# Checking adj's entries: every second row tile by GpSimd and ScalarE, and the diagonal by one strided transfer

## The chip, the cores and the metric

The kernel runs on one core of a Trainium2 chip. The metric is the device time of one execution in microseconds (us). Engines are named as the profile names them: PE is TensorE, DVE is VectorE, ACT is ScalarE, POOL is GpSimd, SP is SyncE, which issues most of the transfers.

## The reference

Four graph layers run one after the other on x, 8 batches of 2048 nodes with 64 features, each as `x = x + layer(relu(layernorm(x)))`. Cut to what matters here:

```python
# x: (8, 2048, 64), adj: (2048, 2048)
h = jnp.maximum(_layernorm(x, axis=-1), 0.0)
x = x + layer0(h, H, adj, ...)     # adj / max(adj.sum(-1), 1) times a projection of h,
                                   # mixed with a hypergraph attention over H
h = jnp.maximum(_layernorm(x, axis=-1), 0.0)
x = x + layer1(h, adj, ...)        # I, A and 2 A A - I as a Chebyshev basis
h = jnp.maximum(_layernorm(x, axis=-1), 0.0)
x = x + layer2(h, adj, ...)        # three rounds of adj times v, each with a small network
h = jnp.maximum(_layernorm(x, axis=-1), 0.0)
x = x + layer3(h, adj, ...)        # attention: softmax over all nodes of adj * leaky_relu(e),
                                   # with adj's diagonal set to 1
```

adj holds only zeros and ones (a sparse random graph whose diagonal is 1). The reference doesn't depend on that, but the kernel has a short path that does.

## The kernel before, in words

The launch has two parts. `start` does the first layernorm, multiplies its result by layer 0's weight in two layouts, and checks the inputs. It ends in a flag: 0 where adj holds only zeros and ones and no node has more neighbours than the short path has room for. `tc.nc.values_load(flag, ...)` reads it, and an `If` takes the short path or the long one (`rest(True)` or `rest(False)`). The whole of each branch is behind that read, on every engine. The profile shows the short path: the first instructions behind the flag start at 111.2 us, and the four layers fill the rest of the span.

Within `start`:

- `layernorm_relu` (called at its end through `norm_parts`, lines 258 to 281) goes over 4 chunks of 512 nodes. A chunk is one 1 MB load `x_ch`, then for each of 4 pairs of batches a matmul with `center`, an ACT Square into `sq` (L264), and a relu into `xr`, in turn on DVE (L267) and on ACT (L269); then a matmul that sums the squares, ACT's square root (L272), DVE's reciprocal (L273), four matmuls that spread the result, and four multiplications by DVE (L553). `xr`, `sq` and `std` have one buffer each, so that a chunk's parts follow those of the chunk before; six banks of PSUM are shared by all matmuls of the stage.
- `features` goes over the same 4 chunks: 4 matmuls 128x512 into `ph` and 4 groups of four 128x128 matmuls into `pn`, each result copied out of PSUM by `copy`, which takes ACT (L172) and DVE (L174) in turn. It starts when the layernorm has given its banks back.
- `check_adj` (L339) goes over the 16 tiles of 128 rows of adj, 1 MB each. SP loads a tile into one of four places (`rows`, two buffers of two tiles, L351). DVE multiplies its 128 columns on the diagonal by the identity and sums them, which gives each node's own entry (`own`, L352). ACT squares the tile into one of two places of `squares`, and sums the squares into `deg` (L357). DVE compares the tile with its squares, writes the comparison over them, and sums it into `same` (L358): an entry is 0 or 1 exactly where it equals its square. `bad` is set where the sum is short of 2048 x 16 over the row's tiles (L362, L363), and `own` becomes deg minus the own entry (L364).
- `count_nodes` turns the degrees of H and adj into counts of nodes above given sizes, and compares them with the room that the short path has (L371 to L407); the rest of `start` joins the three flags over the partitions (L561 to L566).

An instruction of DVE or ACT that also gives a sum shows in the profile with a second, short one that reads the accumulator.

Nothing in the source gives an order between the layernorm, the features and the check. The tile framework arranges each engine's queue when the program is built, and each engine then works through its queue in that order; so check instructions stand among those of the layernorm and the features on SP, ACT and DVE. A place of `rows` is loaded again when its last reader is done, four tiles later, and a place of `squares` is written again two tiles later.

Of the kernel before, what the change touches and what calls it, by code (L numbers as in the profile page):

```python
# [7 lines left out]
F = mybir.dt.float32  # L8
# [4 lines left out]
AF = mybir.ActivationFunctionType  # L13
OP = mybir.AluOpType
# [5 lines left out]
P = 128  # L20
NB = 8
N = 2048
D = 64
NP = NB // 2
NT = N // P
# [102 lines left out]
class Kernel:  # L128
# [210 lines left out]
    def check_adj(self, pool, slots):  # L339


        nc = self.nc
        rows = [slots.tile([P, 2, N], F, name=f"rows{i}", tag=f"q{6 + i}") for i in range(2)]
        squares = slots.tile([P, 2, N], F, name="squares", tag="q8")
        same = pool.tile([P, NT], F, name="same")
        deg = pool.tile([P, NT], F, name="deg")
        own = pool.tile([P, NT], F, name="own")
        junk = pool.tile([P, P], F, name="junk")
        for t in range(NT):
            row, sq = rows[t // 2 % 2][:, t % 2], squares[:, t % 2]  # L350
            nc.sync.dma_start(row, self.a["adj"][t * P : (t + 1) * P])  # L351
            nc.vector.scalar_tensor_tensor(  # L352
                junk, row[:, t * P : (t + 1) * P], 1.0, self.ident, op0=OP.mult, op1=OP.mult,
                accum_out=own[:, t : t + 1],
            )

            nc.scalar.activation(sq, row, AF.Square, accum_out=deg[:, t : t + 1])  # L357
            nc.vector.scalar_tensor_tensor(  # L358
                sq, row, 1.0, sq, op0=OP.mult, op1=OP.is_equal, accum_out=same[:, t : t + 1]
            )  # L360
        bad = pool.tile([P, 1], F, name="bad")
        nc.vector.tensor_reduce(bad, same, axis=AX.X, op=OP.add)  # L362
        nc.vector.tensor_scalar(bad, bad, float(N * NT), None, op0=OP.is_lt)  # L363
        nc.vector.tensor_sub(own, deg, own)  # L364
        return bad, deg, own
# [1985 lines left out]
```

## Time and profile before

| what | us |
|---|---|
| median of 3 runs | 2163.15 |
| the 3 runs | 2158.54, 2163.15, 2169.57 |
| the profiled execution | 2161.53 |
| its span, first to last instruction | 2159.8 |
| DVE busy in the span | 1133.9 |
| ACT busy in the span | 712.2 |
| POOL busy in the span | 706.0 |
| last load of a tile of adj issued by the check | 65.0 |
| the flag's last instruction | 110.35 |

The span is counted from the first instruction to the last; the execution's time has a little around it. The views give start times from the span's start. A row of the timeline reads: start, duration, engine, line, operation, written<-read, shapes, number, and in brackets the idle time of the engine before it and what ended it. Neighbouring instructions of a queue overlap by a tenth or two of a us at their ends, so the cost of one in a row of several is the distance between starts. A group's row gives busy time and mean nanoseconds of one, then the idle time before its instructions and its releasers.

### The profile page before, as it was taken

The page shows a single profiled execution, that of the slowest core. Times are in us where ns is not written, and L with a number is a line of the kernel's source. Part 1 is how long each engine was busy: PE and PEld are TensorE (multiplying, and loading weights), DVE is VectorE, ACT ScalarE, POOL GpSimd, SP SyncE. Part 2 cuts the span into 40 slices and gives each one's busy share as a digit, 9 for nine tenths or more (in the row PEclk, how much of TensorE's full clock was granted, in tenths as well). Part 3 has the DMA queues.
Part 4 walks back from the last instruction along what each step waited for, and adds up shares of the span by engine and source line. Part 5 has one row for each costly group of instructions (what it writes and reads, how often), then busy time and mean ns, then how long its engine had stood idle before and what let it go on. Part 6 is the DMA issues. An engine that isn't in the chain of part 4 may idle for free. (4 is left out here: it accounts for less than half of the span.)

```text
span 2159.8 us, 21301 instructions
## 1 busy us (share of the span) xinstructions
PE 1945.0 (90%) x7466; PEld 1163.0 (54%) x7466; DVE 1133.9 (53%) x1956; ACT 712.2 (33%) x1343; POOL 706.0 (33%) x595
## 2 busy tenths in 40 slices
PE   5879999978879999999999998899999999669885
PEld 1425766642237774353453543677777666445433
DVE  7877677736661123425434255698703222248774
ACT  6412555534543440020110201324335333248400
POOL 0000467754310005707447166011000000177870
PEclk8868999987769999999999999999999999879997
DMA  8230333441024460050230500556444444375665
GB/s 318 82 109 6 103 104 116 134 166 39 40 80 126 123 175 31 5 151 1 73 83 0 122 1 28 169 176 223 167 125 129 135 149 147 132 221 166 177 184 183
DMA packets 108796, 253.64 MB, mean 117 GB/s; under 512 B 20912, under 2 KB 21056, under 8 KB 101376
## 3 DMA queue, kind: packets, MB, share of 16 engines
q1 hardware_dynamic: 89264, 181.45, 27.0%
q0 software_dynamic: 17104, 66.47, 10.1%
q10 hardware_dynamic: 2304, 4.20, 0.5%
q8 instruction: 62, 1.02, 0.2%
q14 instruction: 62, 0.51, 0.1%
HBM read 218.30 MB, written 33.78 MB: 117 GB/s over the span
## 5 line engine op out<-in xcount | busy, mean ns | idle before, releaser
L325 ACT CAST adj<-adj_t 128x512 fp32r<-128x512 f32 x384 | 237.4, 619 | 687.2 <-PE pp L166 354.7
L1408 POOL TENSOR_TENSOR acc<-acc,y 128x512 f32<-128x512 f32 x224 | 277.2, 1269 | 449.2 <-DVE y L1403 449.2
L166 PE MATMUL pp<-adj,hi 128*128 128x512 f32 x1280 | 365.6, 405 | 0.1
L166 PE MATMUL pk<-q,w 128*128 128x512 f32 (+1 forms) x1024 | 358.2, 611 | 4.3 <-ACT q L1376 3.0
L166 PE MATMUL pp<-adj,lo 128*128 128x512 f32 x1280 | 358.7, 400 | 0.0
L166 PEld LDWEIGHTS pp<-adj,hi 128*128 128x128 f32 x1280 | 242.1, 191 | 72.4 <-issue 16.0
L166 PEld LDWEIGHTS pp<-adj,lo 128*128 128x128 f32 x1280 | 244.0, 191 | 56.5
L166 PEld LDWEIGHTS pk<-q,w 128*128 128x128 f32 (+1 forms) x1024 | 136.5, 188 | 214.1 <-issue 167.3
L1403 DVE SCALAR_TENSOR_TENSOR y<-pk,bias,q 128x512 f32<-128x512 f32 x224 | 157.7, 746 | 142.0 <-PE pk L166 135.7
L166 PE MATMUL acc<-q,ident 128*128 128x512 f32 x416 | 202.9, 614 | 26.4 <-DVE q L2138 16.5
L2048 POOL DMA_INDIRECT ring<-f_rows,near x121 | 139.7, 1154 | 67.0 <-issue 28.0
L166 PEld LDWEIGHTS acc<-q,ident 128*128 128x128 f32 x416 | 76.7, 194 | 102.4 <-issue 47.2
L2152 POOL IOTA q<- 128x2048 int32 x1 | 1.8, 1834 | 316.5 <-PE p L166 316.5
L166 PE MATMUL pp<-adj,x_ind_hi 128*128 128x512 f32 x256 | 94.7, 486 | 2.2 <-DVE q L738 1.9
L1840 POOL TENSOR_TENSOR q<-q,beta 128x512 f32<-128x512 f32 x57 | 67.9, 1193 | 54.6 <-DVE beta L1816 30.8
L1403 DVE SCALAR_TENSOR_TENSOR acc<-pk,bias,q 128x512 f32<-128x512 f32 x32 | 22.6, 747 | 119.9 <-PE pk L166 119.9
L166 PE MATMUL bank<-std,from_rows 32*128 32x512 f32 x128 | 46.7, 894 | 41.9 <-DVE std L273 33.8
L2119 DVE TENSOR_TENSOR q<-ring,e 128x1024 f32<-128x1024 f32 x58 | 70.1, 1219 | 8.9 <-PE acc L166 8.8
L166 PE MATMUL pp<-adj,x_ind_lo 128*128 128x512 f32 x256 | 71.7, 399 | 0.0
L1530 POOL DMA_INDIRECT q<-in_adj_dram,order x15 | 19.0, 1270 | 160.3 <-DVE top L1544 133.5
L166 PEld LDWEIGHTS pp<-adj,x_ind_hi 128*128 128x128 f32 x256 | 48.5, 189 | 38.9 <-issue 23.7
L1495 DVE SCALAR_TENSOR_TENSOR q<-p,cols,q 128x512 f32<-128x512 f32 x16 | 12.0, 751 | 108.4 <-PE p L166 107.5
(411 smaller groups left out, 2768.4 us busy)
## 6 DMA issues: line engine op xcount, KB each, us to landing
adj_t<-in_adjT_dram SPq DMA_DIRECT2D x128, 512.0 KB, 4.0
adj_t<-in_adjT_dram SPq DMA_DIRECT2D x128, 256.0 KB, 3.3
rows<-in_adj_dram SPq DMA_DIRECT2D x16, 1024.0 KB, 5.6
q<-x SPq DMA_DIRECT2D x10, 1024.0 KB, 4.9
x<-q SPq DMA_DIRECT2D x9, 1024.0 KB, 3.9
q<-in_embT_dram SPq DMA_DIRECT2D x8, 1024.0 KB, 11.5
x_ch<-in_xT_dram SPq DMA_DIRECT2D x4, 1024.0 KB, 6.3
h_rows<-q SPq DMA_DIRECT2D x16, 256.0 KB, 3.6
```

Of the source, the lines that this page charges most:

```text
L166: self.nc.tensor.matmul(out, lhsT, rhs, start=start, stop=stop)
L325: nc.scalar.copy(moving, at[:, i])
L1403: nc.vector.scalar_tensor_tensor(y, pks[b, half], bias[:, b : b + 1], emb[:, b], op0=OP.add, op1=OP.mult,)
L1408: nc.gpsimd.tensor_add(acc, acc, y)
L1495: nc.vector.scalar_tensor_tensor(x[:, q], p2, self.col("b2"), x[:, q], op0=OP.add, op1=OP.add)
L1530: nc.gpsimd.indirect_dma_start(row, None, self.a["adj"], bass.IndirectOffsetOnAxis(ap=order[:, 1, t : t + 1], axis=0),)
L1840: self.nc.gpsimd.tensor_tensor(x, x, by.unsqueeze(2).to_broadcast([P, NB, D]), op=OP.mult)
L2048: self.nc.gpsimd.indirect_dma_start(to, None, self.kern.f_rows[:], bass.IndirectOffsetOnAxis(ap=index, axis=0))
L2119: nc.vector.tensor_tensor(y.rearrange("n i (b f) -> n i b f", b=NB), block[:, i : i + 2, : NB * D].rearrange("n i (b f) -> n i b f", b=NB) ...
L2152: nc.gpsimd.iota(whole, pattern=[[1, N]], base=0, channel_multiplier=0)
```

## The change

Even tiles are treated as before. For an odd tile, GpSimd subtracts the squares from the tile, in place of the squares, and ScalarE sums the absolute values of the difference into `differ`, which is 0 for a row exactly where all its entries equal their squares. That second ScalarE instruction (`total`) is placed in the source ahead of the load of the tile two further on, which takes the same place of `squares`. At the end, a row of an odd tile with a zero in `differ` counts 2048, as a full comparison did, and is added to the even tile's `same`. The own entries no longer come from the loaded tiles: one transfer issued by GpSimd reads adj's diagonal from memory, 128 x 16 single f32 entries 2049 entries apart, into `own`, at the head of the check. The buffer `junk` is gone, and `same` has half its columns.

```diff
-        same = pool.tile([P, NT], F, name="same")
+        same, differ = (pool.tile([P, NT // 2], F, name=n) for n in ("same", "differ"))
         deg = pool.tile([P, NT], F, name="deg")
         own = pool.tile([P, NT], F, name="own")
-        junk = pool.tile([P, P], F, name="junk")
+        adj = self.a["adj"]
+        nc.gpsimd.dma_start(
+            own, bass.AP(tensor=adj.tensor, offset=adj.offset, ap=[[N + 1, P], [P * (N + 1), NT]])
+        )
+
+        def total(t):
+            sq = squares[:, t % 2]
+            nc.scalar.activation(sq, sq, AF.Abs, accum_out=differ[:, t // 2 : t // 2 + 1])
+
         for t in range(NT):
             row, sq = rows[t // 2 % 2][:, t % 2], squares[:, t % 2]
+            if t % 2 and t > 2:
+                total(t - 2)
             nc.sync.dma_start(row, self.a["adj"][t * P : (t + 1) * P])
-            nc.vector.scalar_tensor_tensor(
-                junk, row[:, t * P : (t + 1) * P], 1.0, self.ident, op0=OP.mult, op1=OP.mult,
-                accum_out=own[:, t : t + 1],
-            )
 
             nc.scalar.activation(sq, row, AF.Square, accum_out=deg[:, t : t + 1])
-            nc.vector.scalar_tensor_tensor(
-                sq, row, 1.0, sq, op0=OP.mult, op1=OP.is_equal, accum_out=same[:, t : t + 1]
-            )
+            if t % 2 == 0:
+                nc.vector.scalar_tensor_tensor(
+                    sq, row, 1.0, sq, op0=OP.mult, op1=OP.is_equal,
+                    accum_out=same[:, t // 2 : t // 2 + 1],
+                )
+            else:
+                nc.gpsimd.tensor_sub(sq, row, sq)
+        total(NT - 1)
         bad = pool.tile([P, 1], F, name="bad")
+        none = pool.tile([P, NT // 2], F, name="none")
+        nc.vector.tensor_scalar(none, differ, 0.0, float(N), op0=OP.is_equal, op1=OP.mult)
+        nc.vector.tensor_add(same, same, none)
         nc.vector.tensor_reduce(bad, same, axis=AX.X, op=OP.add)
```

## The prediction

> **What bounds the kernel now.** The change lies in the first 111 us, before the flag that the program branches on. I first cut that stretch into windows (us; busy time of each engine with its number of instructions; TensorE clock; DMA share; GB/s):
>
> ```profile
> 18.00:82.00 64.00, 40.38 (x101) 13.02 (x102) 63.60 (x88) 42.00 (x55) 0.00 (x0) 0.76 0.69 255
> 82.00:105.30 23.30, 23.30 (x143) 17.54 (x142) 14.01 (x58) 7.85 (x14) 0.00 (x0) 1.00 0.00 1
> 105.30:111.20 5.90, 0.80 (x5) 0.12 (x2) 4.67 (x45) 0.00 (x0) 0.00 (x0) 0.98 0.01 1
> ```
>
> The busy columns are PE, PE's weight load, DVE, ACT, POOL. From 18 to 82 us DVE works 63.60 of 64.00 us: it bounds the layernorm and the check, which share the stretch. From 82 to 105.3 us PE works all the time (the features). Then comes a tail on DVE that makes the flag. POOL does nothing. Next the groups of the first 110 us:
>
> ```profile
> L358 DVE SCALAR_TENSOR_TENSOR squares<-rows,squares 128x2048 f32<-128x2048 f32 x16 | 36.5, 2282 | 1.2 <-ACT squares L357 1.2
> L357 ACT ACTIVATE squares<-rows 128x2048 f32<-128x2048 f32 x16 | 30.5, 1907 | 15.2 <-DVE squares L358 13.9 <-DMA rows<-in_adj_dram 1.3
> L273 DVE RECIPROCAL std<-std 128x512 f32<-128x512 f32 x4 | 13.4, 3349 | 0.7 <-ACT std L272 0.7
> L352 DVE SCALAR_TENSOR_TENSOR junk<-rows,ident 128x128 f32<-128x128 f32 x16 | 4.4, 274 | 1.5 <-DMA rows<-in_adj_dram 1.5
> ```
>
> The check (L352, L358) is about 41 of DVE's us here, and ACT waits 13.9 us for it. How that delays the layernorm is in DVE's timeline of chunk 1 (start, duration):
>
> ```profile
> 34.85 3.34 DVE L273 RECIPROCAL std<-std 128x512 f32<-128x512 f32 x1
> 38.11 0.23 DVE L352 SCALAR_TENSOR_TENSOR junk<-rows,ident 128x128 f32<-128x128 f32 x1
> 38.26 0.08 DVE L352 DVE_READ_ACCUMULATOR junk<-rows,ident 128x1 f32 x1
> 38.26 2.29 DVE L358 SCALAR_TENSOR_TENSOR squares<-rows,squares 128x2048 f32<-128x2048 f32 x1
> 40.47 0.08 DVE L358 DVE_READ_ACCUMULATOR squares<-rows,squares 128x1 f32 x1
> 40.47 0.28 DVE L352 SCALAR_TENSOR_TENSOR junk<-rows,ident 128x128 f32<-128x128 f32 x1
> 40.68 0.08 DVE L352 DVE_READ_ACCUMULATOR junk<-rows,ident 128x1 f32 x1
> 40.68 2.29 DVE L358 SCALAR_TENSOR_TENSOR squares<-rows,squares 128x2048 f32<-128x2048 f32 x1
> 42.90 0.08 DVE L358 DVE_READ_ACCUMULATOR squares<-rows,squares 128x1 f32 x1
> 42.90 2.48 DVE L553 TENSOR_TENSOR q<-xr,bank 128x512 f32<-128x512 f32 x4
> ```
>
> Two whole tiles of the check stand between the reciprocal and the multiplications of L553, which PE's first matmul would have released some 0.7 us after 38.11: L553 is 4.1 us late. The same 4 us is lost in each chunk, and the reciprocals of chunks 1 and 2 begin 2.1 us after their square root. The reciprocals start at 18.34, 34.85, 51.33 and 65.79: periods of 16.5, 16.5 and 14.5, mean 15.8. The last L553 ends at 76.1.
>
> **What the Trainium skill says.** SBUF — State Buffer, section "Who interferes with whom": a VectorE instruction with two inputs in SBUF and a GpSimd instruction that reads SBUF exclude each other; the later one waits for the whole of the earlier. The trace agrees, in a later stage:
>
> ```profile
> 505.43 2.69 POOL L660 TENSOR_TENSOR dt<-tanh 128x1024 f32<-128x1024 f32 x1 [3.54 <-ACT tanh L658]
> 506.44 2.24 DVE L670 TENSOR_TENSOR df<-q,q 128x512 f32<-128x512 f32 x1
> ```
>
> L670 takes 0.69 at other times; here it lasts until 0.56 after POOL's end. GPSIMD Engine Reference, section "3.1 Elementwise": a two-input f32 operation on 2048 elements takes 4497 ns. The trace has none of that length, but 1.26 us for 512 elements (shortest L666) and 2.34 for 1024 (L660): 1.08 more per 512, so 2.34 + 2 x 1.08 = 4.50. ScalarE: Activation LUTs, section "Table sets", has abs in every table set, so Abs adds no table load; no run here shows that yet. DMA: Bandwidth & Descriptors, section "Queues, rings and completion order": each DMA engine takes turns between queues by packets, so a transfer of POOL's gets among SP's; this trace has no such meeting at its start.
>
> **The change part by part.**
>
> DVE loses eight L358, 2.21 from start to start (38.26 to 40.47), 17.7 us, and sixteen L352 at 0.21 (40.47 to 40.68), 3.4: 21.1 us. The two small instructions at the end (0.16 each, like L362 and L364) lie beside the features and cost nothing; if the check were last they'd cost 0.3.
>
> POOL gains eight subtractions of 4.50, 36 us on an idle engine. Unobstructed they're free; what they do to DVE is the lock. In a steady pair of tiles ACT squares the odd one, POOL starts, ACT squares the even one 1.9 later, and DVE's L358 then waits 4.5 - 1.9 = 2.6 and works 2.2: 4.8, with whatever DVE has queued behind it, L553 or the reciprocal, waiting too. Before, a pair took 2 x (2.21 + 0.21) = 4.84. So where the instructions meet, DVE's saving is gone; where they don't, all of it stays.
>
> ACT gains eight Abs at 1.89 (34.68 minus 32.79, two squares in a row): 15.1. It worked 48.7 us between 10 and 82 (42.0 of 64 in the window above, the rest ahead of it), so it comes to 63.8 of 72. Slot 1 of squares has now a chain: square 1.9, subtraction 4.5, Abs 1.9, with 0.2 for hand-overs 8.5 per odd tile, 68 for eight, from about 17 to 85 us; with a wait or two on ACT and the lock, 95. The flag's tail starts at 105 now, so this chain alone isn't last.
>
> What sets the stretch is the layernorm's chain, with ACT's queue in it. Its bare period: reciprocal 3.3, first matmul and four L553 3.1, PE and ACT to the square root's end about 4.9: 11.3. In chunks 2 and 3 the trace has the burst of squares to the square root's end unbroken, 44.92 to 49.27 = 4.4. From the root to the next burst a bare chunk leaves ACT 6.4 to 6.9 us (11.3 less 4.4), and that is where the check's ACT work is queued now, four squares of 1.9. With the same sort of order after the change: square odd, square even, a wait to 6.4 for POOL, Abs, square odd: 10.3, a period of 14.7. With one instruction less behind the wait it is 8.4, a period of 12.8. An instruction on ACT that waits for POOL holds the layernorm's squares behind it, and PE and DVE wait for those. I can't tell from the trace which order is built, and take 14.0, a little nearer to the longer one. Three periods: 3 x (15.8 - 14.0) = 5.4. After the last reciprocal, 65.79 to 76.1 = 10.3 becomes 3.35 + 0.7 + 2.4 and one L358 of 2.2, 8.6: 1.7 saved.
>
> The diagonal's transfer: 2048 pieces of 4 bytes. For its issue on POOL the nearest row is an indirect transfer of 128 rows, 0.95; sixteen times that is 15.2, and POOL isn't wanted before 18: nothing, at either end. For the DMA engines the nearest is hm<-in_H_dram, 2048 runs of 256 bytes, 6.4 us to landing. It would go out near 2 us, together with the first x_ch (issued 2.50, used at 8.02), which the whole chain waits for. Between 0 and 6.4. x_ch is 512 runs of 2 KB, 32 for each of 16 engines, the diagonal 128 for each; turn by turn 32 of those 128, a quarter of 6.4, get in before x_ch is through: I take 1.5. It can't be a gain: nothing is taken out of the queues there.
>
> The features keep their 29.4 us of PE (75.57 to 105.0). Two or three pairs of the check fall beside them; before, two L358 did (76.24 and 79.26) with PE still busy. I put 0, at worst 2 per pair, 6.
>
> The sum: 5.4 + 1.7 - 1.5 = 5.6. All engines wait for the flag, so an earlier flag moves the end by as much. The profiled execution took 2161.5 (span 2159.8), 1.6 below the median 2163.15. 2161.5 - 5.6 = 2155.9; for the median, 2157.6.
>
> **The rivals.**
> Full gain: the built order fits, no lock is met, the period falls to 11.3, 3 x 4.5 = 13.5, and the end to 6.4 (3.9), the transfer hidden: 17.4 less. The squares' chain, 85 to 88, still ends in time. 2146. For it: DVE has no idle time now, and loses a third of its work. Against it: ACT at 63.8 of 72.
> The lock eats it: 4.8 against 4.84 per pair, and the transfer's 1.5: 2164.6. For it: L670 above.
> Slower: two odd tiles' chains are queued on ACT between a root and the next squares, 2 x 8.5 = 17, a period of 21.4, 5.6 more, three times 16.8, less 1.7, plus 1.5: 2179.8. It costs from the point where the gap is over 15.8 - 4.4 = 11.4, that is 1.3 odd tiles per gap. Against it: a full pair a gap is all that eight pairs in some 80 us need.
>
> **How the numbers follow.** Forecast 0.50, full gain 0.18, lock 0.20, slower 0.12. 0.5% is 10.8 us, about what a measurement here can tell from no change (the runs span 2158.5 to 2169.6). Faster by more: the full gain and 0.04 of the forecast, 0.22. Slower by more: two thirds of the last, 0.08. The rest, 0.70, is within. The range runs from the full gain's 2146 to 2170, which takes in the lock with features worsened by 6; half of the full gain and most of the slower case stay out.
>
> **What would show it.** Right: the reciprocals 13 to 15 us apart, POOL's subtraction at 4.5 us or more, some L358 stretched past 2.29, ACT idle on POOL's squares, the last L553 near 70, the flag near 105. Periods under 12 show the full gain; L358 near 4.8 on average shows the lock; ACT's wait for POOL above 20 us with squares of the layernorm behind it shows the slower case. A first x_ch later than 9.5 shows the transfer mis-sized. I'd be wrong altogether if the flag came early and the end didn't.

## The result and the profile after

The changed kernel takes 2177.59 us, median of 11 runs (2170.59 to 2184.35), against 2162.8 for the kernel before in as many runs beside it. The ratio is 1.007, with a 95% interval from 1.0052 to 1.0088: slower, by some 15 us, where the forecast was 5.6 us faster. The profiled execution took 2179.18 us, 17.6 more than the one of before, with a span of 2177.4.

First, where the time went. The flag's last instruction starts at 127.61 us in place of 110.35, 17.3 later. That is all but 0.3 of the difference of the two profiled executions; behind the flag nothing changed (2049.5 and 2049.8 us). So the three windows of before are cut again at the same events: first reciprocal to last multiplication, features, tail (busy columns PE, PE's weight load, DVE, ACT, POOL):

```profile
19.60:93.00 73.40, 39.24 (x85) 11.17 (x85) 55.65 (x57) 54.08 (x66) 33.35 (x8) 0.74 0.61 220
93.00:122.50 29.50, 29.50 (x158) 21.68 (x159) 15.91 (x45) 10.59 (x17) 3.22 (x1) 0.90 0.00 1
122.50:128.40 5.90, 0.86 (x4) 0.09 (x2) 4.67 (x45) 0.00 (x0) 0.00 (x0) 0.83 0.01 1
```

Features and tail are as long as before, 29.5 and 5.9 us. The first window grew, and in it DVE now works 55.65 of 73.40 us: it has idle time again, and the stretch got longer. Whatever bounds it now, it isn't DVE's work.

The layernorm's reciprocals start at 19.61, 39.38, 58.47 and 77.61 (before: 18.34, 34.85, 51.33, 65.79), periods of 19.8, 19.1 and 19.1, mean 19.3 where it was 15.8. The last multiplication ends at 92.9 (76.1). So: first reciprocal 1.3 later, three periods 10.5, the end after the last reciprocal 15.3 instead of 10.3, so 5.0, and the features 0.5: 17.3.

Next the groups of the first 128 us that answer to those of before:

```profile
L371 POOL TENSOR_TENSOR squares<-rows,squares 128x2048 f32<-128x2048 f32 x8 | 36.6, 4572 | 56.7 <-ACT squares L364 56.7
L366 DVE SCALAR_TENSOR_TENSOR squares<-rows,squares 128x2048 f32<-128x2048 f32 x8 | 22.4, 2798 | 6.3 <-ACT squares L364 6.3
L356 ACT ACTIVATE squares<-squares 128x2048 f32<-128x2048 f32 x8 | 15.2, 1905 | 18.8 <-POOL squares L371 18.8
L379 DVE TENSOR_TENSOR own<-deg,own 128x16 f32<-128x16 f32 x1 | 3.4, 3446 | 0.0
```

The sizes were as forecast: the subtraction 4572 ns, the sum (L356) 1905, the comparison (L366) 2282 before and 2798 on the mean now, because two of the eight met a subtraction (4.82 us at 66.17, 4.03 at 34.81). The new row is the 18.8 us that ACT waits in front of L356 for POOL, in five waits: one in each of the three gaps between a root and the next chunk's squares (4.62, 4.88 and 2.74), two after the last root. ACT's timeline in the gap ahead of chunk 2, between the root of chunk 1 (L272) and chunk 2's squares (L264), shows one of them (start, duration; in brackets the idle time ahead of the instruction):

```profile
38.03 0.69 ACT L272 ACTIVATE std<-bank,eps 128x512 f32<-128x512 f32 x1 [1.25 <-PE bank L166]
38.62 1.90 ACT L356 ACTIVATE squares<-squares 128x2048 f32<-128x2048 f32 x1
...
40.51 1.90 ACT L364 ACTIVATE squares<-rows 128x2048 f32<-128x2048 f32 x1
...
42.40 1.90 ACT L364 ACTIVATE squares<-rows 128x2048 f32<-128x2048 f32 x1
...
49.27 1.91 ACT L356 ACTIVATE squares<-squares 128x2048 f32<-128x2048 f32 x1 [4.88 <-POOL squares L371]
...
51.30 1.91 ACT L364 ACTIVATE squares<-rows 128x2048 f32<-128x2048 f32 x1
...
53.21 1.06 ACT L264 ACTIVATE sq<-bank 128x512 f32<-128x512 f32 x2
```

The subtraction that it waits for, from POOL's timeline:

```profile
44.47 4.77 POOL L371 TENSOR_TENSOR squares<-rows,squares 128x2048 f32<-128x2048 f32 x1 [7.78 <-ACT squares L364]
```

From the root's end, 38.72, to the next squares, 53.21, are 14.5 us. In them ACT sums an odd tile, squares an even one, squares the next odd one, and then has the sum of that odd tile at its queue's head. POOL began that subtraction at 44.47 and takes 4.77, so ACT stands for 4.88 us, and the layernorm's squares stand behind it; when their turn comes they start without a wait of their own. The gap ahead of chunk 3, from 58.43 to 72.82, holds six instructions of the check (square, sum, square, square, sum, square), 14.4 us. The one ahead of chunk 1 holds four and a wait, 12.2 us, and a fifth stands among chunk 1's squares.

Last, what a subtraction does to a small instruction. The timeline of all engines at the end of the layernorm:

```profile
83.03 4.95 DVE L386 TENSOR_SCALAR least<-deg 128x16 bf16<-128x16 f32 x7
83.06 4.51 POOL L371 TENSOR_TENSOR squares<-rows,squares 128x2048 f32<-128x2048 f32 x1 [5.55 <-ACT squares L364]
...
87.90 0.67 DVE L568 TENSOR_TENSOR q<-xr,bank 128x512 f32<-128x512 f32 x1
```

Seven instructions on 16 elements took 4.95 us, one of them 4493 ns, where the median of the eleven between 83.0 and 88.7 is 161: it ended with POOL's subtraction. The multiplication behind them, which starts the features, came 4.9 us later than DVE's turn for them.

### The profile page after: what moved, and what is told of

Its sections match the earlier page's. It is cut to its first block, busy times and chain, and to the rows that moved or that the text cites. A ratio compares the mean times of both kernels' runs of the same rounds, so it can differ in the third digit from the quotient of the medians.

```text
span 2177.4 us, 21278 instructions
## 1 busy us (share of the span) xinstructions
PE 1944.5 (89%) x7466; PEld 1161.2 (53%) x7466; DVE 1123.2 (52%) x1910; ACT 728.2 (33%) x1359; POOL 745.5 (34%) x604
## 5 line engine op out<-in xcount | busy, mean ns | idle before, releaser
L166 PE MATMUL acc<-q,ident 128*128 128x512 f32 x416 | 203.0, 614 | 28.6 <-DVE q L2153 18.3
L1545 POOL DMA_INDIRECT q<-in_adj_dram,order x15 | 19.1, 1270 | 158.8 <-DVE top L1559 132.4
L1855 POOL TENSOR_TENSOR q<-q,coef 128x512 f32<-128x512 f32 x57 | 59.6, 1045 | 26.3 <-DVE q L1878 21.2
```

What stands on the lines that cost most here:

```text
L166: self.nc.tensor.matmul(out, lhsT, rhs, start=start, stop=stop)
L1545: nc.gpsimd.indirect_dma_start(row, None, self.a["adj"], bass.IndirectOffsetOnAxis(ap=order[:, 1, t : t + 1], axis=0),)
L1855: self.nc.gpsimd.tensor_tensor(x, x, by.unsqueeze(2).to_broadcast([P, NB, D]), op=OP.mult)
```

## The experiments

Sixteen kernels were run. Since the difference lies ahead of the flag, each is read by three numbers of its profile, beside the ratio of its time to that of the kernel before: the mean period of the reciprocals, the last multiplication's end, and the time from the first reciprocal to the flag ("stretch"), which leaves out how early the first loads came. The ratio is of many runs beside the kernel before; the other three are of one execution each. In those of the experiments the part behind the flag took 2059 to 2077 us (e14 aside), against 2050 for the first two kernels, so only what lies ahead of the flag is compared, and differences of one us between stretches carry no weight here.

| kernel | ratio, 95% interval | period | last mult. ends | stretch |
|---|---|---|---|---|
| before | 1 | 15.8 | 76.1 | 92.0 |
| after | 1.007 [1.0052, 1.0088] | 19.3 | 92.9 | 108.0 |
| e1 diagonal alone | 0.9996 [0.9976, 1.0016] | 15.7 | 76.9 | 89.9 |
| e2 split alone | 1.0085 [1.0065, 1.0104] | 20.2 | 94.3 | 110.9 |
| e3 no sum | 1.0029 [1.0008, 1.0051] | 16.5 | 82.8 | 99.3 |
| e4 sum waits for nobody | 1.0076 [1.0052, 1.01] | 17.5 | 87.3 | 103.4 |
| e5 odd comparison left out | 1.0007 [0.9992, 1.0022] | 14.4 | 72.2 | 89.0 |
| e6 no sum, POOL writes | 1.0015 [0.9996, 1.0033] | 14.6 | 74.4 | 88.6 |
| e7 POOL writes | 1.0016 [1.0, 1.0032] | 15.7 | 77.8 | 93.8 |
| e8 DVE subtracts | 1.0012 [0.9997, 1.0027] | 16.3 | 79.3 | 94.6 |
| e9 one-input comparison | 1.0065 [1.0041, 1.0089] | 18.4 | 89.2 | 104.6 |
| e10 POOL writes, same order | 1.0105 [1.0054, 1.0156] | 18.9 | 87.5 | 104.9 |
| e11 small instructions late | 1.0068 [1.0037, 1.0099] | 19.2 | 90.7 | 106.9 |
| e12 old comparison, order by hand | 0.9988 [0.997, 1.0007] | 15.7 | 75.2 | 88.5 |
| e13 one pair per gap | 1.0049 [1.0029, 1.0068] | 15.9 | 75.9 | 97.3 |
| e14 half a subtraction | (see there) | 15.9 | 80.1 | 94.2 |
| e15 no check | 0.9955 [0.9939, 0.9971] | 13.4 | 65.6 | 81.1 |
| e16 after, held order | 1.006 [1.0041, 1.0079] | 18.4 | 89.6 | 104.5 |

Where an edit says "order held", ACT's and DVE's instructions of the layernorm and the check were tied to a written list; without one an edit can make the build arrange the queues anew. For e9, e10, e14 and e16 it is the changed kernel's list in all but one point: it takes the squares in the tiles' own order, while the changed kernel has, ahead of chunk 2, an even tile's square ahead of an odd tile's. So e9, e10 and e14 are measured against e16. In such a list q and L are ACT's and DVE's own instructions of layernorm and features, S a square, A a sum, E a comparison.

### The two halves of the change: e1, e2

e1 is the kernel before with the diagonal's transfer, e2 the changed kernel without it.

```diff
 e1, against before
-        junk = pool.tile([P, P], F, name="junk")
+        adj = self.a["adj"]
+        nc.gpsimd.dma_start(
+            own, bass.AP(tensor=adj.tensor, offset=adj.offset, ap=[[N + 1, P], [P * (N + 1), NT]])
+        )
...
-            nc.vector.scalar_tensor_tensor(
-                junk, row[:, t * P : (t + 1) * P], 1.0, self.ident, op0=OP.mult, op1=OP.mult,
-                accum_out=own[:, t : t + 1],
-            )
 e2, against after: these lines the other way round
```

> The diagonal's transfer alone: DVE compares all 16 tiles as before, and no longer reads the diagonal. If the transfer's only cost is at the front (first squares 0.8 us later in the changed kernel than before) and DVE was the bound, DVE gets back sixteen times 0.21 = 3.4 us less 0.8: 1 to 4 us faster than before. If the transfer is what hurts (rival: it disturbs the loads of the layernorm's chunks), 1 to 5 us slower than before, with the first squares later than 11 us.

> The other part alone: odd tiles by GpSimd and ScalarE, the diagonal by DVE from the loaded tiles as before. Theory of ACT's queue (a subtraction on GpSimd stands between two ACT instructions, and the layernorm's squares wait behind both): as slow as the whole change or 1 to 3 us slower than it, 15 to 18 us over before, reciprocals 19 us apart. If the transfer were the cause, within 4 us of before.

e1 can't be told from before (flag at 109.72; the gain of 1 to 4 us that was expected of it did not show), e2 has the whole loss (flag at 128.90). The transfer is innocent, and with it gone the split is, if anything, worse. The first reciprocal is at 19.79 in e1 and 18.05 in e2, against 18.34 before and 19.61 after: the transfer costs 1.3 to 1.6 us at the start in these pairs (in e5 and e6, which carry it too, the first reciprocal is at 18.96 and 20.73, so the figure isn't sharp), and the sixteen small diagonal products that it saves give that back (e1's stretch is 2.1 shorter).

### Is it ACT's sum, or its wait? e3, e4, e6

```diff
 e3: the sums of odd tiles are left out (differ is set to 0 at the start, as in e5, e6 and e15)
-            nc.scalar.activation(sq, sq, AF.Abs, accum_out=differ[:, t // 2 : t // 2 + 1])
+            pass
 e4: the sum reads the loaded tile, not the difference
-            nc.scalar.activation(sq, sq, AF.Abs, accum_out=differ[:, t // 2 : t // 2 + 1])
+            row = rows[t // 2 % 2][:, t % 2]
+            nc.scalar.activation(
+                spare, row, AF.Abs, scale=0.0, accum_out=differ[:, t // 2 : t // 2 + 1]
+            )
 e6: as e3, and
-                nc.gpsimd.tensor_sub(sq, row, sq)
+                for i in range(2):
+                    nc.gpsimd.memset(sq, 0.0)
```

> The whole change without the second ScalarE instruction of odd tiles: GpSimd still subtracts, nobody sums the difference (the check of odd tiles is left out). Takes both ACT's load of 8 x 1.9 and its waits for GpSimd away[...]. Theory of ACT's queue: the periods fall below 15.8 and the time is 3 to 10 us below before. Theory of the lock (GpSimd's eight subtractions hold DVE up): periods stay at 18 to 19 and the time at least 10 us above before.

> The whole change, but the second ScalarE instruction reads the loaded tile times 0 into a spare buffer instead of GpSimd's difference (so the check of odd tiles is left out): ACT's load is the same, its wait for GpSimd is gone. If the waits (18.8 us in 5 places) are the cause: most of the loss is back, within 4 us of before. If the load is (8 x 1.9 in the gaps between square root and next squares): still 8 to 12 us above before. If the lock on DVE is: as slow as the change.

> The kernel without Abs, with GpSimd writing the odd place twice (two memsets of 128x2048, about 4 us together) in place of the subtraction; the odd tiles' check is left out. GpSimd reads nothing, so by the skill's rule DVE's two-input comparisons don't exclude it. If the lock is what costs the kernel without Abs its 8 us: comparisons at 2.2 to 2.4 us each and the flag at 98 to 106. If it is GpSimd's time between two squares: as late as without Abs, 115 to 120.

None of the three isolates one cause, and they are worth showing for that: e3's period (16.5) and e6's flag (109.33) fall between what the two sides expected, and e4's ratio is as slow as the change while its flag (122.89) is 4.7 us earlier. Without the sums the loss is more than halved (e3). But with the sums in place and free of POOL it is still there in the ratio (e4: 1.0076, stretch 4.6 shorter than after): ACT waits 7.9 us for POOL all the same, now in front of squares, which need the place that POOL is reading. A wait taken off one instruction came back at the next one in the same queue. In e3 the squares wait 8.8 us for POOL, and the comparisons meet the subtractions far more often:

```profile
L368 DVE SCALAR_TENSOR_TENSOR squares<-rows,squares 128x2048 f32<-128x2048 f32 x8 | 27.8, 3470 | 1.2 <-ACT squares L366 1.2
```

3470 ns is 1.2 us over a free comparison, eight times: 9.5 us of lock. With POOL writing in place of subtracting (e6), it is 2282 again and the stretch 10.7 shorter than e3's. Part of that is not the lock, as two writes take 3.7 us and not 4.7.

### How much is DVE's relief worth? e5, e15, e12

```diff
 e5: the odd tiles are squared, but not compared: no subtraction, no sum
-            nc.scalar.activation(sq, sq, AF.Abs, accum_out=differ[:, t // 2 : t // 2 + 1])
+            pass
...
-                nc.gpsimd.tensor_sub(sq, row, sq)
+                pass
 e15: as e5, and no squares and no comparisons of even tiles (deg and same are constants)
-            nc.scalar.activation(sq, row, AF.Square, accum_out=deg[:, t : t + 1])
-                nc.vector.scalar_tensor_tensor(
-                    sq, row, 1.0, sq, op0=OP.mult, op1=OP.is_equal,
-                    accum_out=same[:, t // 2 : t // 2 + 1],
-                )
+                pass
 e12: before with the diagonal's transfer, a second pair of places for squares, order held,
      DVE's other instructions of the check put behind the last multiplication:
+    "qqqqSqqqSSSqqqqqqqSSSqqqqqqqSSSqqqqqqqSSSqqSqqSqqSqqqqqqqqqq",
+    "LLELLLLLELLEELLLLLELLEELLLLLELLEELLLLLELLELLELLELLELLELLLLLL",
```

> The whole change without the odd tiles' comparison: they are squared for the degrees, and neither subtracted nor summed (their check is left out). What is left is DVE's relief alone: 8 comparisons and 16 readings of the diagonal less, 21 us of DVE, no lock, no wait for GpSimd. If DVE's work was the bound of the stretch, as the profile of before was read: the flag at 92 to 98 us, 12 to 18 us before the 110 of the kernel before. If the order of ACT's queue or the layernorm's own chain is the bound: flag at 103 or later.

> No GpSimd in the check: the diagonal's transfer and the old comparison on DVE, with four places for squares and the queues ordered by hand so that no comparison stands between a reciprocal and its multiplications (one after them, two after the relus), and six comparisons in the features. If comparisons ahead of the multiplications are what delays the layernorm (4 us a chunk in the profile of before), the periods fall to 13 to 14.5 and the flag to 98 to 104. If the layernorm's own chain is the bound, as the kernel of e5 suggests with its 14.5: 106 to 112.

> The check's arithmetic is left out (no squares, comparisons, subtractions and sums; the rows and the diagonal are still loaded), so that the layernorm stands alone. Its bare period: 11.3 us if the prediction's sum was right (reciprocals 34 us apart from first to last); 13 to 13.5 if the first multiplication after a reciprocal comes 2 us and more later and not 0.7 (39 to 40.5 us from first to last). Flag 104 to 108 us.

e5 takes from DVE what the change takes, about 21 us, and puts nothing in its place. The flag comes 2.4 us earlier (107.96), and the time can't be told from before's. In the order that was built for it, that is what the relief alone is worth. It is no ceiling: ACT waits 5.0 us for tiles of adj in e5, and e6 and e12, with more work, have stretches as short (88.6 and 88.5). Without the check's arithmetic (e15; adj and the diagonal are still loaded) the flag is at 98.60, earlier than the 104 to 108 that were expected and 11.75 before that of the kernel before, 10.5 of it at the last multiplication; the ratio says 0.9955. So that arithmetic moves the flag of the kernel before by 11.75 us in all, though DVE spends 41 us on it. What limits then is seen in e15's DVE, one whole period:

```profile
30.68 3.35 DVE L273 RECIPROCAL std<-std 128x512 f32<-128x512 f32 x1 [1.87 <-ACT std L272]
36.19 2.48 DVE L568 TENSOR_TENSOR q<-xr,bank 128x512 f32<-128x512 f32 x4 [2.16 <-PE bank L166]
...
44.09 3.35 DVE L273 RECIPROCAL std<-std 128x512 f32<-128x512 f32 x1 [1.87 <-ACT std L272]
```

With nothing in the way the first multiplication starts 2.16 us after the reciprocal's end, not 0.7, and the period is 13.4 us, not 11.3. In the kernel before the reciprocal shown ends at 38.19 and the multiplications start at 42.90; with the bare 2.16 in between they are 2.6 us late, not 4.1. e12 tries the old comparison in an arrangement of my own, and comes out where before is; none of the arrangements with a check in them beats it by what the measurement can tell. It doesn't show that comparisons ahead of the multiplications are harmless, for it moved the delay: its multiplications come 2.16 us after a reciprocal, but two comparisons now stand ahead of the next reciprocal, which starts 2.6 us after its root has ended:

```profile
48.26 0.69 ACT L278 ACTIVATE std<-bank,eps 128x512 f32<-128x512 f32 x1 [0.65 <-PE bank L172]
...
51.51 3.35 DVE L279 RECIPROCAL std<-std 128x512 f32<-128x512 f32 x1
```

### GpSimd's length or ACT's extra work? e7, e8, e14, e16

```diff
 e7: POOL writes only, twice
-                nc.gpsimd.tensor_sub(sq, row, sq)
+                for i in range(2):
+                    nc.gpsimd.memset(sq, 0.0)
 e8: DVE does the subtraction
+                nc.vector.tensor_sub(sq, row, sq)
 e14: POOL subtracts half of the columns, order held
+                h = slice(0, N // 2)
+                nc.gpsimd.tensor_sub(sq[:, h], row[:, h], sq[:, h])
 e16: nothing else; held for e9, e10, e14 and e16:
+    "qqqqSqqqSASSqSqqqqqqASSASqqqqqqqSASSASqqqqqqqSASSASqAqqqqqqqqqqqqqqq",
+    "LLELLELLLLELLELLLLLLLELLELLLLLELLELLLLLLLLLLLLLLLLLL",
```

> The whole change with GpSimd's two memsets in place of the subtraction, and Abs behind them (the odd tiles' check is left out): ACT's load and its waits for GpSimd stay, the lock goes. If ACT's queue is the main cause, the flag is at 120 or later; if the lock is, at 112 or earlier.

> DVE subtracts in place of GpSimd, ScalarE sums as in the change: no GpSimd, no lock, ACT's load of 15.2 stays, DVE works as many passes as before. If GpSimd (its 4.5 us and its lock) is the cause: the flag between 108 and 114, near before. If the 8 more instructions on ACT are: 120 or later.

> The change with its own order of ScalarE and VectorE held, GpSimd subtracting only half of each odd tile's columns, so about 2.3 us instead of 4.5 (the other half of an odd tile's comparison is left out). Theory (GpSimd's length in a fixed order is the cost): ScalarE's wait for GpSimd falls from 18.8 us below 9, periods 16 to 17.5, flag 114 to 119 us, ratio 1.001 to 1.004. Rival (ScalarE's eight more instructions are the cost): flag above 122 us, ratio above 1.005.

> The control for the kernels with a held order: the changed kernel with nothing left out and the written list for ScalarE and VectorE. The list takes the squares in the tiles' own order, while the changed kernel's build puts, in the gap of chunk 2, tile 6's square ahead of tile 5's, so that GpSimd starts there 1.9 us later. Theory (GpSimd's length is the cost, the lock a small part): it is 1 to 3 us better than the changed kernel, stretch from the first reciprocal to the flag 105 to 107.5 us, ScalarE's waits for GpSimd 16 to 18 us, so that GpSimd's length (against half a subtraction, 94.2) is worth 11 to 13 us, and the lock (against writes that read nothing, 104.9, and against one input, 104.6) 0 to 3. Rival (holding the order does something by itself): a stretch below 103 or above 110 us.

These settle it. e8 has all of ACT's extra work, and from the root of chunk 0 on the check stands in ACT's queue as in the changed kernel, but for one sum that changed places with a square ahead of chunk 1 and the last sum, which stands two copies later beside the features. Only the subtraction is DVE's, 2280 ns. The stretch is 94.6, 13.4 shorter than after (the flag, 114.50, is half a us past the range expected), and ACT waits 4.0 us ahead of the sums (in total, times, the longest):

```profile
ACT squares L356 <- DVE squares L371: 4.0, 4, 2.7
```

From the first reciprocal to the last multiplication DVE is busy 55.5 us, as in the changed kernel, but of 59.3 and not of 73.3: it has less idle time, and the layernorm runs faster.

e14 comes to the same by the other way: GpSimd keeps the job but does half of each tile, 2376 ns. The waits of ACT for POOL, in e16 and in e14 (us in total, times, the longest):

```profile
ACT squares L362 <- POOL squares L381: 17.0, 5, 4.6
```

```profile
ACT squares L362 <- POOL squares L382: 6.4, 5, 2.5
```

The same queue and the same five waits, 10.6 us less of them, and a stretch of 94.2 against 104.5: 10.3 less, where 11 to 13 were expected. (Of e14 only the part up to the flag is read, as its flag sends the program down the other branch, 5694.92 us; so it has no ratio here.) e16 against the changed kernel shows what the place of one square does. Ahead of chunk 2, POOL's tile is squared first, POOL starts 4.0 us after the root and not 5.8, ACT waits 2.73 there and not 4.88, and the stretch is 3.5 shorter (the period from chunk 1 to chunk 2 is 15.7, not 19.1); the ratios, 1.006 and 1.007, are too close to tell. So of the 16.0 us that the stretch grew, 3.5 hang on that square's place, 10.3 on GpSimd's length beyond 2.4 us, and 2.2 are the rest (94.2 less 92.0): ACT's eight more instructions and the waits that remain, less what DVE's relief gives back.

e7's flag, 113.20, lies between its two cases: the order is not a given. Where the build had two writes to place, it arranged ACT's queue anew, with fewer sums in the gaps; ACT waited 8.3 us and the stretch was 93.8. For a subtraction it made nearly the same order whether GpSimd (4.5 us) or DVE (2.3 us) was to do it. That it took GpSimd's subtraction for a short one is my inference from these orders; no run shows the build's prices.

### The lock and the small instructions: e9, e10, e11

```diff
 e9: the even tiles' comparison gives way to a reduction with one input (same is scaled
     to 2048 afterwards), order held
-                nc.vector.scalar_tensor_tensor(
-                    sq, row, 1.0, sq, op0=OP.mult, op1=OP.is_equal,
-                    accum_out=same[:, t // 2 : t // 2 + 1],
+                i = nc.vector.tensor_reduce(
+                    same[:, t // 2 : t // 2 + 1], sq, axis=AX.X, op=OP.max
 e10: POOL writes for as long and reads nothing, order held
-                nc.gpsimd.tensor_sub(sq, row, sq)
+                nc.gpsimd.memset(sq, 0.0)
+                nc.gpsimd.memset(sq, 0.0)
+                nc.gpsimd.memset(sq[:, : N // 2], 0.0)
 e11: hm, and with it L386's instructions, wait for the check
+        zero = pool.tile([P, 1], F, name="zero")
+        nc.vector.tensor_scalar(zero, adj_deg[:, NT - 1 :], 0.0, None, op0=OP.mult)
-        nc.vector.tensor_scalar(hm, hm, 0.0, None, op0=OP.is_gt)
+        nc.vector.tensor_scalar(hm, hm, zero, None, op0=OP.is_gt)
```

> The whole change with the queues of ACT and DVE held to the order that they have in it, and DVE's comparison of even tiles replaced by a reduction over the squares alone: one input in SBUF, so that GpSimd's subtraction (the same, 4.5 us) no longer excludes it (the even tiles' check is left out). What GpSimd's slowness costs through ACT's queue stays, what the lock costs on the comparisons goes. Lock: flag at 118 to 122, the first three periods under 18. ACT's queue behind the subtraction: flag at 123 or later.

> The whole change with ACT's and DVE's queues in its order, and GpSimd writing 2.5 times 128x2048 (about 4.5 us, nothing read) in place of the subtraction; the odd tiles' check is left out. Compared with e7 it has the change's order and its length on GpSimd. If the lock was what e7 gained, the flag stays at 113 to 116. If e7 gained by its other order and its 0.9 us shorter GpSimd work, the flag is at 121 or later.

> The whole change, with the counts over H made to wait for the check's last result, so that no small bf16 instruction of DVE (L386) stands behind a subtraction of GpSimd ahead of the last multiplications. If those 4.95 us at 83 us are on the path: flag at 122 to 124, last multiplication 4 to 5 us earlier. If not: 127.

Both e9 and e10 take the lock off the comparisons, one on DVE's side and one on POOL's: DVE's eight instructions take 2268 and 2274 ns on the mean, where e16's comparisons take 3122. The rows of e9 and e16:

```profile
L375 DVE TENSOR_REDUCE same<-squares 128x1 f32<-128x2048 f32 x8 | 18.1, 2268 | 8.8 <-ACT squares L372 8.8
```

```profile
L375 DVE SCALAR_TENSOR_TENSOR squares<-rows,squares 128x2048 f32<-128x2048 f32 x8 | 25.0, 3122 | 7.7 <-ACT squares L372 7.7
```

That is 6.8 us less work on DVE, and the stretch is 104.6 and 104.9 against e16's 104.5. Before e16 was run I had read e9's and e10's gain over the changed kernel, 3 us, as the lock's price. It is the held order's. In this queue the lock on the comparisons costs nothing: DVE has the time, and ACT stands for POOL anyhow (17.0 us in e9, 18.3 in e10). So e14's gain isn't the lock's, though its comparisons too are shorter (2377). e9 is the clean case of the two. In e10 the small instructions, which no list holds, stand elsewhere, the last multiplication ends 2.7 us sooner after the first reciprocal than in e16, and from there to the flag it takes 3.0 longer. e11 shortens the stretch by 1.1: the 4.95 us at 83.03 are gone, but the comparisons are stretched more (3112 ns). The last multiplication comes 2.2 us earlier, not the 4 to 5 expected, and its ratio can't be told from the changed kernel's.

### An order that allows for 4.5 us: e13

The changed kernel with all its instructions, in an order by hand, one pair of tiles per gap (sum of the last odd tile, square, square):

```diff
+    "qqqqSqqqSSqqASSqqqqqASSqqqqqqqASSqqqqqqqASSASSqqqASSqqqqASqqqqAqqqqq",
+    "LLELLLLLELLELLLLLLLELLLLLLLELLLLLELLLELLLLELLLLLLLLL",
```

> The whole change with all its instructions, but ScalarE's and VectorE's order of the stretch written by hand: one pair of tiles per gap between a root and the next squares (sum of the odd tile before, square of the odd tile, square of the even tile), the other pairs beside the features, and a comparison never ahead of a reciprocal that could run. Theory (the order planned for a short subtraction makes ScalarE wait for GpSimd inside the gap): ScalarE's wait for GpSimd in the gaps is near zero, periods 13.5 to 15.5, last multiplication by 74 to 78 us, flag 106 to 112 us, ratio 0.997 to 1.001. Rival (GpSimd's reading costs wherever it stands, by the lock with the comparisons, and ScalarE has too much work): periods above 16.5, flag above 116 us, ratio above 1.003.

ACT waits for POOL in no gap, the two undisturbed periods are 14.9 and 12.6 (the first is 20.3, since I had put a sum and two squares among chunk 1's squares), and the layernorm ends at 75.9, as before the change, with the same subtractions of 4.6 us. That part of the expectation held, though the mean period, 15.9, is over its 15.5: it is not that GpSimd works, but that ACT's queue has a wait for it in the gap. The flag and the ratio did not come out: 117.43 and 1.0049, the numbers I had given the rival, by a third way. The three pairs that didn't fit in the gaps went beside the features, and held up ACT's copies there. Lines of its timeline of all engines:

```profile
92.17 1.91 ACT L372 ACTIVATE squares<-rows 128x2048 f32<-128x2048 f32 x1 [3.27 <-DMA rows<-in_adj_dram]
...
94.08 0.56 ACT L178 COPY q<-pn 128x512 f32<-128x512 f32 x1
...
94.70 1.49 PE L172 MATMUL pn<-ww,q 128*128 128x128 f32 x11 [3.54 <-ACT q L178]
```

A square waits 3.27 us for its tile's load, the copy behind it waits with it, and PE 3.54 us for the copy. The features end near 112.5, 36.5 us after they began, not 29.4. Whether some order of these instructions would end as early as before stays open, and so does what the best order could gain: e5's 2.4 us are those of one order, and 11.75 are what leaving the check's arithmetic out altogether brings.

## Why the prediction was wrong

**The failed step** is the period: "square odd, square even, a wait to 6.4 for POOL, Abs, square odd: 10.3, a period of 14.7", of which I took 14.0. The mechanism is the one in that sentence. But the gaps ahead of chunks 2 and 3 hold five and six instructions of the check, not four, and ahead of chunk 2 the sum of an odd tile and the square of an even one stand first, so that POOL starts 5.8 us after the root and ACT's wait for it ends at 49.27, 10.6 after the root, not 6.4. The gap is 14.5, not 10.3, the period 19.3. Three times 5.3 is 16.0 of the 22.9 us between the sum's -5.6 and the measured +17.3. It was in the rivals as the slower case (gap over 11.4 us, 2179.8, chance 0.12), a time near the measured one by luck, with a gap of 17 us in place of 14.5 and the end mis-sized the other way, and argued away with "a full pair a gap is all that eight pairs in some 80 us need". On the mean that holds. This queue wasn't built to the mean: parts of two odd tiles' chains went into a gap, with one wait in each gap.

**The end after the last reciprocal** is 15.3, not 8.6: 6.7 more. Two comparisons lie in it where I counted one, and the small instructions of L386 stuck behind a subtraction. I had looked for the lock on the large comparisons alone. The Trainium skill, SBUF — State Buffer, "Who interferes with whom", names more than the two-input forms: tensor_scalar and copy can contend too, in the modes that use both ports. The runs agree in that a tensor_scalar of 16 elements took 4493 ns here and a copy of 16 elements 4.38 us in e13, both to the end of a subtraction; that they ran in such a mode no run here shows. e6's expectation leans on the same section: a GpSimd instruction that only writes doesn't contend with a two-input one, and with writes the comparisons took 2282 ns in e6 and 2274 in e10.

**What bounds it** was misread, and the full gain rested on it. DVE was taken for the bound, at 63.60 of 64.00 us busy. In the order that was built its instructions do follow one another without a gap; what was missed is how close the next limit lies. e5 removes a third of that work, and the flag comes 2.4 us earlier, with periods of 14.4. Much of DVE's work stood where the chain waits anyhow: without the check (e15) DVE is busy 27.5 of the 48.1 us from the first reciprocal to the last multiplication. The chain's 11.3 us were put together from parts with a first multiplication 0.7 us after the reciprocal; e15 has 2.16 and 13.4. The full gain's 17.4 us was more than leaving out the whole of the check's arithmetic brings (11.75), and so out of reach for sharing it out.

**Lock.** The price, 2.6 us where the two meet, was right: 4.82 at 66.17. Two comparisons of eight paid it, not every pair, and by e9 it isn't on the path. In e3, where ACT had no sums to wait with, it was paid more (9.5 us on the comparisons).

**ACT's and POOL's sizes.** Sum 1905 ns against 1.89, subtraction 4572 against 4.50, which the Trainium skill's GPSIMD Engine Reference, "3.1 Elementwise", has as 4497: the shortest here took 4.49. Abs brought no table load: ACT has two ahead of the flag, as before.

**The diagonal.** Issued in 1.37 us on POOL, near the lower end of 0.95 to 15.2. x_ch was used at 8.85 in place of 8.05, and the first reciprocal was 1.3 later, against 1.5: right as far as these pairs tell, as was that the features keep their length (0.5 against 0) and that an earlier or later flag moves the end by as much (17.3 and 17.6).

**The signs named in advance** pointed to the slower case without reaching it: ACT's wait for POOL was to be above 20 us with the layernorm's squares behind it, and is 18.8, of which 12.2 stand ahead of squares of the layernorm. The range, 2146 to 2170, left the slower case out, as its 0.12 let it.

## What to carry to other kernels

An engine that is busy all the time in a stretch may leave little to gain: take its filler away in thought, add up the bare chain with each wait from the trace, and see how close the next limit lies before sharing the filler out. Where work moves to a slower engine and its result comes back to an engine in the chain, find which instruction waits for it and what stands behind that one in the queue; an average of work per gap doesn't say, the order does. In such a trial hold the order of the queues while one length is changed, and run the unchanged kernel in the held order too: without that control, 3 us of order passed for a lock.

## What was not expected of the hardware

- A GpSimd subtraction of 128 x 2048 holds up even the smallest DVE instructions: 16 elements into bf16 for 4.5 us, L379 (16 elements, two inputs) for 3.45. It doesn't hold up all: beside subtractions of the changed kernel four multiplications with one input in PSUM took 2.48 us, as in e15 (at 44.88), and the reduction L396 took 1.21 (at 74.04; 1.22 in e15).
- GpSimd's write of 128 x 2048 f32 takes 1.80 to 1.86 us, 2.5 times less than its subtraction, and leaves DVE's comparison at 2.27 to 2.28.
- DVE can stretch POOL as well: in e4 the subtraction took 5334 ns on the mean, and 6.04 us where a comparison had begun 0.56 us ahead of it.
- 2048 pieces of 4 bytes, 8196 bytes apart, were in SBUF 4.6 us after their issue.
